# Convolution taps on TensorE from four shifted copies per channel, the output bias on TensorE, dt's weights on four row groups

## The chip, the cores and the metric

The kernel runs on one core of one Trainium2 chip. The metric is the device time of one execution in microseconds; the median of the runs shown is compared. A profile of one execution stands beside the times. Engines are named as in the profile: PE is TensorE's matmul, PEld its weight load, DVE is VectorE, ACT is ScalarE, POOL is GpSimd, and SP is SyncE, which issues nearly all DMAs here, one after the other from one queue.

## The reference

It is one decoder layer in float32 on x of shape (8, 512, 512): a Mamba block, a cross-attention block and a mixture of 32 experts, each followed by an addition and a layer norm. What the change touches is the Mamba block's front and the attention's output:

```python
xz = _layernorm(x) @ in_proj_w                    # 512 -> 2 * 1024
x_main, z = jnp.split(xz, 2, axis=-1)
x_conv = causal_depthwise_conv1d(x_main, conv_w)  # 4 taps per channel, 1024 channels
x_main = silu(x_conv + conv_b)
dt, B, C = jnp.split(x_main @ x_proj_w, [32, 48], axis=-1)
dt = softplus(dt @ dt_proj_w + dt_proj_b)
h_t = exp(A * dt_t) * h_(t-1) + dt_t * B_t * x_t  # 16 states per channel, 512 steps
y = (sum over states of h * C + x_main * D) * silu(z)
out = res_scale * (y @ out_proj_w) + residual
...
attention output: att @ Wo + bo, added to its input
```

The convolution at time t is the sum over k of conv_w[c, k] * x_main[t - 3 + k, c], with zeros before the start of a sequence.

## The kernel before, in words

The program has three parts: `layers` (Mamba, attention, the shared expert and the routing), `experts` and `finish`. `layers` holds a loop over 16 chunks, two of 256 time steps for each of the 8 batches. A chunk has 32 steps (q, g, jj): q counts four groups of 256 channels, g four groups of states, jj two halves. In a step, DVE multiplies dt*x by B (L494), scans along time (L501) and multiplies by C (L510). ACT computes the decays exp(A*dt) for the next step (L480) and copies the state carried in (L488). After the second step of a pair, PE sums the states of both h tiles with four products of 32 columns each into `py` (L521, `fold` is the weight). The h tiles come from a ring of six; a tile is free for its next use when PE has read it.

Everything else is woven into these steps. Chunk i+1's front (its layer norm, transposes, projections, convolution, silu and x_proj) runs at fixed values of k, the step's number in chunk i: norm at 8, transposes at 11, `convolve` at 12, 14, 17 and 20 for q = 0 to 3, silu at 22, x_proj at 23, `prepare` of its first q at 25. The attention and the rest of the previous batch come from a list (`units`), which `work(k)`'s estimates spread over the steps. Each step is cut into thirds. A part may return a rest, which `settle` runs at the next call; `wait` holds it back three thirds. The compiler's scheduler may still reorder instructions on an engine where the data allow it, and the order is fixed when the program is built.

`convolve` projects 256 channels on PE (L343, eight products of 128x256 into PSUM). `first_tap` copies them to the SBUF tile `xp` (L363), which has three columns in front for the previous chunk's tail: POOL clears them (L360) or copies them in (L362), and saves the new tail (L365). ACT then writes the first tap with its bias to `xs` (L369), once for each of two sets of 128 channels. `other_taps` adds three taps to each on DVE (L377, six instructions for a convolution). `xp` is a single tile; `prepare` uses it too, under the name `l`.

`x_proj` (L400) multiplies all channels; `spill` copies the result to `xd` (L406) and sends the B and C rows to DRAM (L408), from where `bcast` spreads them over partitions (L418). `prepare` makes dt: two products of 32 rows (L437), then ACT (L447 to L453) and DVE (L457 to L460). `repeat` spreads dt and dt*x over the partitions by DMA (L428). `pieces` streams the projection weights (L159).

In the attention, `output` multiplies by Wo through `dense` (L750), and `add_up` adds its input (L913) and the bias `bo`, which stands on all partitions (L914). `biases` first folds bv @ Wo into `bo` (L1049).

Of the kernel before, what the change touches and what calls it, by code (L numbers as in the profile page):

```python
# [88 lines left out]
def layers(ctx, tc, a, x1d, filld, based, xbuf):  # L89
# [31 lines left out]
    p2 = ctx.enter_context(tc.tile_pool(name="l_p2", bufs=2))  # L121
    p3 = ctx.enter_context(tc.tile_pool(name="l_p3", bufs=2))
    dp = ctx.enter_context(tc.tile_pool(name="l_dram", bufs=2, space=DRAM))
    psm = ctx.enter_context(tc.tile_pool(name="l_psm", bufs=2, space=PSUM))
    psy = ctx.enter_context(tc.tile_pool(name="l_psy", bufs=1, space=PSUM))
    pss = ctx.enter_context(tc.tile_pool(name="l_pss", bufs=2, space=PSUM))
# [46 lines left out]
    piece = begun(pieces())  # L173
    lnw = const("lnw", [P, DC], a["ln_w"])
    lnb = const("lnb", [P, DC], a["ln_b"])
    cw = const("cw", [P, CC, 4], rows(a["conv_w"]))
    cb = const("cb", [P, CC], a["conv_b"])
    w_x = const("w_x", [P, CC, RANK + 2 * NST], rows(a["x_proj_w"]))
    w_dt = const("w_dt", [RANK, DI], a["dt_proj_w"])
    b_dt = const("b_dt", [P, CC], a["dt_proj_b"])  # L180
    dpar = const("dpar", [P, CC], a["D_param"])
    rs = const("rs", [P, 1], a["res_scale"].partition_broadcast(P))
    bq = cp.tile([P, DC], F32, name="l_bq")
    bk = cp.tile([P, DC], F32, name="l_bk")
    bv = cp.tile([P, DC], F32, name="l_bv")
    bo = cp.tile([P, D], F32, name="l_bo")
    wg = cp.tile([P, DC, E], F32, name="l_wg")

    aneg = cp.tile([P, CC, NQ, NG], F32, name="l_aneg")
# [14 lines left out]
    for at, sign in ((0, 1), (NQ - 1, -1)):  # L204
        nc.gpsimd.affine_select(
            out=fold, in_=fold if at else ones[:, 0:QP], pattern=[[-NQ * sign, QP]], compare_op=ALU.is_ge, fill=0.0,
            base=at, channel_multiplier=sign,
        )
    before = cp.tile([P, P], F32, name="l_before")
    nc.gpsimd.affine_select(  # L210
        out=before, in_=ones, pattern=[[1, P]], compare_op=ALU.is_gt, fill=0.0, base=0, channel_multiplier=-1
# [29 lines left out]
    va = cp.tile([P, SC, NH // 2, 3 * HD], F32, name="l_va")  # L241
    nc.gpsimd.memset(va[:, :, :, HD : 2 * HD], 1.0)

    def big(tag, name):
        return p1.tile([P, SC * (ROW if tag == "s1" else D)], F32, tag=tag, name=name)

    def quad(tag, name):
        return big(tag, name)[:, 0 : DC * S].rearrange("p (c t) -> p c t", c=DC)

# [13 lines left out]
    def later_constants():  # L263

        nc.sync.dma_start(
            aneg.rearrange("p c j g -> p (c j) g"),
            a["A_log"].rearrange("(b c) (s g) -> (c s) b g", c=QP, s=NQ),
        )
        for i in range(NPB):
            for r0 in (HD + 1, 2 * HD + HD + 1):  # L270
                nc.sync.dma_start(
                    kas[i][r0 : r0 + 1, :].rearrange("p (c t) -> p c t", c=DC),
                    ones[0:1, :].unsqueeze(1).to_broadcast([1, DC, P]),
                )
        nc.sync.dma_start(bq, a["bq"])
        nc.sync.dma_start(bk, a["bk"])
        nc.sync.dma_start(bv, a["bv"].rearrange("(c p) -> p c", p=P))
        nc.sync.dma_start(bo, a["bo"].partition_broadcast(P))
        nc.sync.dma_start(wg, rows(a["wg"]))


# [4 lines left out]
    def wait(part):  # L286

        return (clock[0] + 3 if clock else 0), part

    def behind(part):  # L290

# [60 lines left out]
    def convolve(t, q, f):  # L352

        c0 = 2 * q
        ps = project(f, "ps_x")

        def first_tap():
            xp = mp.tile([P, 2, T + 3], F32, tag="xp", name="xp")
            if t == 0:
                nc.gpsimd.memset(xp[:, :, 0:3], 0.0)  # L360
            else:
                nc.gpsimd.tensor_copy(xp[:, :, 0:3], conv_tail[:, c0 : c0 + 2, :])  # L362
            nc.scalar.copy(xp[:, :, 3:], ps)  # L363
            if t < S // T - 1:
                nc.gpsimd.tensor_copy(conv_tail[:, c0 : c0 + 2, :], xp[:, :, T : T + 3])  # L365
            f["xs"][q] = xs = mp.tile([P, 2, T], F32, tag="xs", name="xs", bufs=5)
            for i in range(2):
                c = c0 + i
                nc.scalar.activation(  # L369
                    xs[:, i, :], xp[:, i, 0:T], AF.Identity, bias=cb[:, c : c + 1], scale=cw[:, c, 0:1]  # L370
                )

            def other_taps():
                for i in range(2):
                    acc = xs[:, i, :]
                    for k in range(1, 4):
                        nc.vector.scalar_tensor_tensor(  # L377
                            acc, xp[:, i, k : k + T], cw[:, c0 + i, k : k + 1], acc, ALU.mult, ALU.add
                        )

            return wait(other_taps)

        return first_tap

    def gate_x(q, f):
        if q == 0:
# [10 lines left out]
    def x_proj(f):  # L397
        psd = psm.tile([P, 2, T], F32, tag="mm", name="ps_d")
        for c in range(CC):
            nc.tensor.matmul(  # L400
                psd[0:64, 0, :], w_x[:, c, :], f["xs"][c // 2][:, c % 2, :], start=(c == 0), stop=(c == CC - 1)
            )

        def spill():
            f["xd"] = xd = mp.tile([64, T], F32, tag="xd", name="xd")
            nc.scalar.copy(xd, psd[0:64, 0, :])  # L406
            f["scr"] = scr = dp.tile([2 * NST, T], F32, tag="scr", name="scr")
            nc.sync.dma_start(scr, xd[RANK : RANK + 2 * NST, :])  # L408

        return spill  # L410

# [20 lines left out]
    def prepare(q, f):  # L432

        ps = psm.tile([P, 2, T], F32, tag="mm", name="ps_dt")
        for i in range(2):
            c = 2 * q + i
            nc.tensor.matmul(  # L437
                ps[:, i, :], w_dt[:, c * P : (c + 1) * P], f["xd"][0:RANK, :], start=True, stop=True
            )

        def exponentials():
            u = mp.tile([P, 2, T], F32, tag="u", name="u")
            dt = mp.tile([P, 2, T], F32, tag="dt", name="dt")
# [26 lines left out]

            return wait(both)

        return exponentials
# [10 lines left out]
    def carry(t, q, g, jj):  # L484

        last = state[:, q, g, jj].unsqueeze(2)
        h = mp.tile([P, NB, T + 1], F32, tag="h", name="h", bufs=6)
        nc.scalar.copy(h[:, :, 0:1], last if t else nothing)  # L488
        return h

# [253 lines left out]
            todo.append((3.4, lambda j=j: keys(j), False))  # L744
        return todo

    def dense(lhs, rhs):
        ps = psm.tile([P, S], F32, tag="mm", name="ps_p")
        for dc in range(DC):
            nc.tensor.matmul(ps, lhs(dc), rhs(dc), start=(dc == 0), stop=(dc == DC - 1))  # L750
        return ps

    def units(b):
# [148 lines left out]
        def output(lt):  # L902
# [4 lines left out]
            if lt + 1 < SC:  # L907
                fetch(lt + 1)
            w, attT = loaded["Wo"], st["attT"]
            pp = dense(lambda dc: attT[:, dc, lt * P : (lt + 1) * P], lambda dc: w[:, dc, :])  # L910

            def add_up():
                nc.vector.tensor_tensor(xr, pp, xr, ALU.add)  # L913
                nc.vector.tensor_tensor(st["x2"][lt], xr, bo, ALU.add)  # L914
                if lt == SC - 1:
                    return layernorm(nc, sm, st["x2"], st["x2"], "ln3")

# [113 lines left out]
    def biases():  # L1031
# [12 lines left out]
        for dc in range(DC):  # L1044
# [1 line left out]
            nc.tensor.matmul(  # L1046
                psb, rep[:, dc * P : (dc + 1) * P], loaded["Wo"][:, dc, :], start=(dc == 0), stop=(dc == DC - 1)
            )
        nc.vector.tensor_tensor(bo, bo, psb, ALU.add)  # L1049

    chunks = [(b, t) for b in range(B) for t in range(S // T)]
    steps = [(q, g, jj) for q in range(CC // 2) for g in range(NG) for jj in range(2)]
# [13 lines left out]

    def work(k):

        front = 6.9 if k in (2, 3) else 3.4 if 4 <= k < 8 or k in (12, 14, 17, 20, 23) else 1.0 if k in (11, 25) else 0.0
        return 1.2 + front  # L1070

    f = {"xt": x0}
# [26 lines left out]
    for i, (b, t) in enumerate(chunks):  # L1099
# [7 lines left out]
        for k, (q, g, jj) in enumerate(steps):  # L1107
# [20 lines left out]
            if k == 25 and after:  # L1128
                part(prepare, 0, nf)
            if after:  # L1130
                if k == 8:
                    part(norm_x, nf)
                if k == 11:
                    for j in range(DC // 2):
                        part(flip_x, j, nf)
                if k in (12, 14, 17, 20):
                    part(convolve, after[1], (12, 14, 17, 20).index(k), nf, first=(k == 12))
                if k == 22:
                    parts.append((finish_silu, *nf["xs"].values()))
                if k == 23:  # L1140
                    part(x_proj, nf)
            if side and (k >= 4 or t and k < 2):
# [421 lines left out]
```

## Time and profile before

| what | us |
|---|---|
| median of 3 runs | 5407.47 (5407.45 to 5411.06) |
| the profiled execution's own time | 5406.28 |
| its span from the first to the last instruction | 5404.6 |
| DVE busy in the span | 4235.9 (78%) |
| PE busy in the span | 4672.4 (86%) |
| ACT busy in the span | 2593.6 (48%) |

The mean granted TensorE clock is 0.935. The span falls into the start (to about 57 us), the scan loop (to about 3490), the rest of the last batch (to about 3800), the experts (to about 5340) and the final layer norm. In rows of the groups by line, the numbers after the count are the busy time of the group in us and the mean of one instruction in ns, then the engine's idle time before them and what ended it. In rows of waits they are the total in us, the number of waits and the longest. The busy time of a group counts overlapping instructions once. A float32 product stands as two PE records.

### The profile page before, as it was taken

The numbers are of one execution on the slowest core, as the hardware profiler recorded it, in microseconds if no ns is written. First come the engines' busy times: TensorE is split into PE (matmuls) and PEld (weight loads), VectorE is DVE, ScalarE is ACT, GpSimd is POOL, SyncE is SP. The second block draws the span as 40 slices with busy tenths as digits, with TensorE's granted clock in tenths as the row PEclk, the third lists the DMA queues.
The fourth block names the chain that finished last, engine by engine and source line by source line (L and its number), as shares of the span: only waits on it lengthen the run. The fifth ranks groups of instructions, "written<-read, shape, count | busy, mean of one in ns | idle before, by whom it ended". The sixth has DMA issues, their size and how long they took to land. (4 is left out here: it accounts for less than half of the span.)

```text
span 5404.6 us, 53991 instructions
## 1 busy us (share of the span) xinstructions
PE 4672.4 (86%) x17320; PEld 2476.6 (46%) x17320; DVE 4235.9 (78%) x5369; ACT 2593.6 (48%) x5726; POOL 570.3 (11%) x426
## 2 busy tenths in 40 slices
PE   6768889788888988988888888789999999999994
PEld 3324234234333423433333342333677777777773
DVE  7999899989989989898998998943566555665554
ACT  5566565565656556566565655523222222222223
POOL 1000002002000200200200020011111111111111
PEclk8879989999999999999999999899999999999997
DMA  8875346345444634634544463342344444544544
GB/s 236 266 224 146 87 96 208 81 114 176 114 104 117 197 77 109 189 98 107 174 125 100 117 200 78 91 146 66 103 128 127 123 117 118 127 127 121 129 115 144
DMA packets 486427, 719.03 MB, mean 133 GB/s; under 512 B 117137, under 2 KB 200625, under 8 KB 484096
## 3 DMA queue, kind: packets, MB, share of 16 engines
q1 hardware_dynamic: 450128, 627.16, 41.1%
q0 software_dynamic: 33280, 76.90, 7.5%
q10 hardware_dynamic: 2736, 11.54, 0.5%
q8 instruction: 137, 2.24, 0.2%
q14 instruction: 146, 1.20, 0.1%
HBM read 391.24 MB, written 165.05 MB: 103 GB/s over the span
## 5 line engine op out<-in xcount | busy, mean ns | idle before, releaser
L480 ACT ACTIVATE l_da<-rep,l_aneg 128x256 f32<-128x256 f32 x2048 | 895.0, 501 | 941.8 <-DVE h L501 877.0
L501 DVE TENSOR_TENSOR_SCAN h<-l_da,h 128x1028 f32<-128x1028 f32 x512 | 1166.0, 2292 | 20.3 <-ACT l_da L480 17.7
L494 DVE TENSOR_TENSOR h<-rep,bc 128x1024 f32<-128x1024 f32 x512 | 614.7, 1218 | 103.1 <-PE py L521 84.6
L510 DVE TENSOR_TENSOR h<-h,bc 128x1024 f32<-128x1024 f32 x512 | 619.5, 1217 | 2.1
L521 PE MATMUL py<-h,l_fold 128*32 128x512 f32 x2048 | 368.3, 644 | 113.4 <-DVE h L510 96.5
L813 PE MATMUL ps_s<-l_ka,l_qa 64*128 64x512 f32 x1024 | 325.6, 707 | 137.8 <-DVE mx L815 137.6
L1314 PE MATMUL ps_h<-xT,w 128*128 128x320 f32 x1536 | 435.8, 433 | 0.0
L1394 POOL DMA_INDIRECT based<-y,xe x160 | 255.5, 1597 | 1309.9 <-ACT y L1417 630.0
L1335 DVE TENSOR_TENSOR hT<-ps_h,p 128x320 f32<-128x320 f32 x128 | 62.9, 492 | 378.5 <-PE ps_h L1314 378.5
L815 DVE TENSOR_REDUCE mx<-ps_s 128x2 f32<-128x1024 f32 x256 | 310.2, 1217 | 58.5 <-PE ps_s L813 58.3
L1314 PEld LDWEIGHTS ps_h<-xT,w 128*128 128x128 f32 x1536 | 292.5, 191 | 118.3 <-issue 0.4
L855 PE MATMUL po<-eT,l_va 128*64 128x512 f32 x1024 | 301.5, 670 | 47.6 <-ACT eT L843 43.1
L839 PE MATMUL ps_t<-l_qa,l_ka 64*128 64x512 f32 x1024 | 308.4, 674 | 23.8 <-ACT eT L843 23.1
L843 ACT ACTIVATE eT<-ps_t 128x1024 f32<-128x1024 f32 x256 | 259.0, 1015 | 128.8 <-PE ps_t L839 128.5
L688 POOL DMA_INDIRECT xbuf<-x2t,dest x128 | 217.2, 1697 | 860.4 <-DVE dest L679 760.8
L1314 PE MATMUL ps_h<-t,s 128*128 128x320 f32 x1024 | 286.1, 432 | 0.0
L343 PE MATMUL ps_z<-xnT,wm 128*128 128x256 f32 x1024 | 238.0, 388 | 30.0 <-DVE o L561 24.3
L750 PE MATMUL ps_p<-x2T,wa 128*128 128x512 f32 x512 | 241.5, 626 | 18.1 <-ACT hT L944 10.4
L552 PE MATMUL po<-wm,zs 128*128 128x512 f32 x512 | 244.7, 632 | 13.8 <-DVE z L957 11.9
L343 PE MATMUL ps_x<-xnT,wm 128*128 128x256 f32 x1024 | 246.5, 393 | 4.5 <-ACT xnT L332 2.5
L343 PEld LDWEIGHTS ps_z<-xnT,wm 128*128 128x128 f32 x1024 | 194.6, 193 | 93.0 <-DVE o L561 37.5
L343 PEld LDWEIGHTS ps_x<-xnT,wm 128*128 128x128 f32 x1024 | 196.1, 195 | 80.5 <-issue 43.8
(232 smaller groups left out, 7170.4 us busy)
## 6 DMA issues: line engine op xcount, KB each, us to landing
w<-in_w SPq DMA_DIRECT2D x93, 1024.0 KB
wm<-in_in_proj_w SPq DMA_DIRECT2D x128, 512.0 KB
rep<-dt SPq DMA_DIRECT2D x256, 256.0 KB
rep<-dtx SPq DMA_DIRECT2D x256, 256.0 KB
xbuf<-zero SPq DMA_DIRECT2D x32, 1362.5 KB
xe<-xbuf SPq DMA_DIRECT2D x32, 1362.5 KB
wm<-in_out_proj_w SPq DMA_DIRECT2D x64, 512.0 KB
wa<-in_sw SPq DMA_DIRECT2D x24, 1024.0 KB
```

Source lines behind the costliest of these rows:

```text
L343: nc.tensor.matmul(ps[:, i, :], w[:, dc, i * P : (i + 1) * P], f["xnT"][:, dc, :], start=(dc == 0), stop=(dc == DC - 1),)
L480: nc.scalar.activation(da[:, n, 1:], dt[:, j, i, :], AF.Exp, scale=aneg[:, 2 * q + i, 2 * jj + j, g : g + 1])
L494: nc.vector.tensor_tensor(h[:, :, 1:], dtx.rearrange("p j i t -> p (j i) t"), f["bc", g][0], ALU.mult)
L501: nc.vector.tensor_tensor_scan(flat, da.rearrange("p n t -> p (n t)"), flat, 0.0, ALU.mult, ALU.add)
L510: nc.vector.tensor_tensor(h[:, :, 0:T], h[:, :, 1:], f["bc", g][1], ALU.mult)
L521: nc.tensor.matmul(f["py"][j * QP : (j + 1) * QP, :, :], fold, hs[j // 2][:, 2 * (j % 2) : 2 * (j % 2) + 2, 0:T], start=False, stop=g == N ...
L813: nc.tensor.matmul(ps[:, j, :], qa[r, lt * P : (lt + 1) * P], ka[r, :], start=True, stop=True)
L815: return lambda: nc.vector.tensor_reduce(mx[:, lt, :].unsqueeze(2), ps, AX.X, ALU.max) and None
L839: nc.tensor.matmul(ps[:, j, :], ka[r, kc * P : (kc + 1) * P], qa[r, :], start=True, stop=True)
L843: nc.scalar.activation(eT, ps, AF.Exp)
L855: nc.tensor.matmul(po[j * 2 * HD : (j + 1) * 2 * HD, :], va[:, kc, i, j * HD : (j + 2) * HD], eT[:, j, :], start=(kc == 0), stop=(kc == SC ...
L1314: nc.tensor.matmul(ps, w[:, n, r * P : (r + 1) * P], x[:, n, :], start=not more and n == 0, stop=n == 1, skip_group_check=more,)
```

## The change

The three DVE taps and ACT's first tap of a convolution are replaced. After the copy to `xp`, eight DMAs (`shifted`) make four copies of each channel, shifted by 0 to 3 columns, on four neighbouring partitions: a tile `xk` holds 32 channels times four shifts on its 128 partitions, four times over. Five thirds of a step after that, `summed` multiplies each by a 128x32 matrix that has the four taps of a channel in its column: eight products of 256 columns into PSUM. ACT then adds the bias while it copies the result to `xs`. The matrices are built once at the start: the weights are gathered by partition, multiplied by the 0/1 matrix `fold` and stored in DRAM, and a convolution loads its 128 KB from there.

The output bias becomes a fifth product of `dense`: 32 rows, of which one row of the weight `only` is 1, against rows of `qas[0]`, one of which holds the bias. dt's weights stand on four groups of 32 partitions instead of one, dt's input is copied to all four by three DMAs, and `prepare(q)` uses group q. The ring of h tiles has five tiles instead of six. The front of the next chunk starts a step earlier, and `convolve` runs at 11, 13, 15 and 17.

```diff
-    cw = const("cw", [P, CC, 4], rows(a["conv_w"]))
-    w_dt = const("w_dt", [RANK, DI], a["dt_proj_w"])
+    w_dt = cp.tile([P, 2 * P], F32, name="l_w_dt")
+    for q in range(CC // 2):
+        nc.sync.dma_start(w_dt[q * RANK : (q + 1) * RANK, :], a["dt_proj_w"][:, 2 * q * P : 2 * (q + 1) * P])
...
-    bo = cp.tile([P, D], F32, name="l_bo")
+    bo_row = slice(HD, 2 * HD)
+    only = cp.tile([P, P], F32, name="l_only")
...
+    nc.gpsimd.affine_select(
+        out=only, in_=ones, pattern=[[0, P]], compare_op=ALU.is_ge, fill=0.0, base=1 - 2 * HD, channel_multiplier=1
+    )
+    tapsd = dram1.tile([CC // 2, P, 2 * NQ, QP], F32, name="tapsd")
+    by_tap = big("s1", "by_tap")
+    nc.sync.dma_start(by_tap[:, 0 : DI // QP], a["conv_w"].rearrange("(n c) k -> (c k) n", c=QP))
+    blocks = by_tap[:, D : D + DI].rearrange("p (n m) -> p n m", m=QP)
+    nc.vector.tensor_tensor(
+        blocks,
+        by_tap[:, 0 : DI // QP].unsqueeze(2).to_broadcast(blocks.shape),
+        fold.unsqueeze(1).to_broadcast(blocks.shape),
+        ALU.mult,
+    )
+    nc.sync.dma_start(tapsd.rearrange("q p n m -> p q (n m)"), blocks.rearrange("p (q n) m -> p q (n m)", q=CC // 2))
...
+    def later(part, thirds):
+
+        return (clock[0] + thirds if clock else 0), part
...
         ps = project(f, "ps_x")
-
-        def first_tap():
+        taps = mp.tile([P, 2, NQ, QP], F32, tag="taps", name="taps")
+        nc.sync.dma_start(taps.rearrange("p i j m -> p (i j m)"), tapsd[q].rearrange("p n m -> p (n m)"))
+
+        def shifted():
...
-            f["xs"][q] = xs = mp.tile([P, 2, T], F32, tag="xs", name="xs", bufs=5)
+            xks = []
             for i in range(2):
-                c = c0 + i
-                nc.scalar.activation(
-                    xs[:, i, :], xp[:, i, 0:T], AF.Identity, bias=cb[:, c : c + 1], scale=cw[:, c, 0:1]
-                )
-
-            def other_taps():
-                for i in range(2):
-                    acc = xs[:, i, :]
-                    for k in range(1, 4):
-                        nc.vector.scalar_tensor_tensor(
-                            acc, xp[:, i, k : k + T], cw[:, c0 + i, k : k + 1], acc, ALU.mult, ALU.add
-                        )
-
-            return wait(other_taps)
-
-        return first_tap
+                xk = mp.tile([P, NQ, T], F32, tag="xk", name="xk", bufs=2)
+                for j in range(NQ):
+                    src = xp[j * QP : (j + 1) * QP, i, 0:T]
+                    four = bass.AP(src.tensor, src.offset, [list(src.ap[0]), [1, 4], [1, T]])
+                    nc.sync.dma_start(xk[:, j, :], four)
+                xks.append(xk)
+            return later(lambda: summed(xks), 5)
+
+        def summed(xks):
+            pc = psm.tile([P, 2, T], F32, tag="mm", name="ps_c")
+            for i in range(2):
+                for j in range(NQ):
+                    nc.tensor.matmul(
+                        pc[j * QP : (j + 1) * QP, i, :], taps[:, i, j, :], xks[i][:, j, :], start=True, stop=True
+                    )
+
+            def out():
+                f["xs"][q] = xs = mp.tile([P, 2, T], F32, tag="xs", name="xs", bufs=5)
+                for i in range(2):
+                    nc.scalar.activation(
+                        xs[:, i, :], pc[:, i, :], AF.Identity, bias=cb[:, c0 + i : c0 + i + 1]
+                    )
+
+            return 0, out
+
+        return shifted
...
-            f["xd"] = xd = mp.tile([64, T], F32, tag="xd", name="xd")
-            nc.scalar.copy(xd, psd[0:64, 0, :])
+            f["xd"] = xd = mp.tile([P, T], F32, tag="xd", name="xd")
+            row = p3.tile([P, D], F32, tag="row", name="bcrow")[RANK : RANK + 2 * NST, 0:T]
+            nc.scalar.copy(row, psd[RANK : RANK + 2 * NST, 0, :])
             f["scr"] = scr = dp.tile([2 * NST, T], F32, tag="scr", name="scr")
-            nc.sync.dma_start(scr, xd[RANK : RANK + 2 * NST, :])
+            nc.sync.dma_start(scr, row)
+            nc.scalar.copy(xd[0:RANK, :], psd[0:RANK, 0, :])
+            for r in range(1, CC // 2):
+                nc.sync.dma_start(xd[r * RANK : (r + 1) * RANK, :], xd[0:RANK, :])
...
-            c = 2 * q + i
-            nc.tensor.matmul(
-                ps[:, i, :], w_dt[:, c * P : (c + 1) * P], f["xd"][0:RANK, :], start=True, stop=True
-            )
+            r = slice(q * RANK, (q + 1) * RANK)
+            nc.tensor.matmul(ps[:, i, :], w_dt[r, i * P : (i + 1) * P], f["xd"][r, :], start=True, stop=True)
...
-        h = mp.tile([P, NB, T + 1], F32, tag="h", name="h", bufs=6)
+        h = mp.tile([P, NB, T + 1], F32, tag="h", name="h", bufs=5)
...
-            pp = dense(lambda dc: attT[:, dc, lt * P : (lt + 1) * P], lambda dc: w[:, dc, :])
+            pp = dense(
+                lambda dc: attT[:, dc, lt * P : (lt + 1) * P], lambda dc: w[:, dc, :], (only[bo_row], qas[0][bo_row])
+            )
 
             def add_up():
-                nc.vector.tensor_tensor(xr, pp, xr, ALU.add)
-                nc.vector.tensor_tensor(st["x2"][lt], xr, bo, ALU.add)
+                nc.vector.tensor_tensor(st["x2"][lt], pp, xr, ALU.add)
...
-                if k == 8:
+                if k == 7:
                     part(norm_x, nf)
-                if k == 11:
+                if k == 10:
...
-                if k in (12, 14, 17, 20):
-                    part(convolve, after[1], (12, 14, 17, 20).index(k), nf, first=(k == 12))
+                if k in (11, 13, 15, 17):
+                    part(convolve, after[1], (11, 13, 15, 17).index(k), nf, first=(k == 11))
```

More of the change, by code (lines that the diff above doesn't have):

```diff
@@ L123, in layers @@
     dp = ctx.enter_context(tc.tile_pool(name="l_dram", bufs=2, space=DRAM))
+    dram1 = ctx.enter_context(tc.tile_pool(name="l_dram1", bufs=1, space=DRAM))
     psm = ctx.enter_context(tc.tile_pool(name="l_psm", bufs=2, space=PSUM))
@@ L208, in layers, with big @@
         )
+    nc.gpsimd.affine_select(
+        out=only, in_=ones, pattern=[[0, P]], compare_op=ALU.is_ge, fill=0.0, base=1 - 2 * HD, channel_multiplier=1
+    )
+    def big(tag, name):
+        return p1.tile([P, SC * (ROW if tag == "s1" else D)], F32, tag=tag, name=name)
+    tapsd = dram1.tile([CC // 2, P, 2 * NQ, QP], F32, name="tapsd")
[9 more added lines that the diff above has]
+    nc.sync.dma_start(tapsd.rearrange("q p n m -> p q (n m)"), blocks.rearrange("p (q n) m -> p q (n m)", q=CC // 2))
     before = cp.tile([P, P], F32, name="l_before")
@@ L242, in layers @@
     nc.gpsimd.memset(va[:, :, :, HD : 2 * HD], 1.0)
-    def big(tag, name):
-        return p1.tile([P, SC * (ROW if tag == "s1" else D)], F32, tag=tag, name=name)
     def quad(tag, name):
@@ L277, in later_constants @@
         nc.sync.dma_start(bv, a["bv"].rearrange("(c p) -> p c", p=P))
-        nc.sync.dma_start(bo, a["bo"].partition_broadcast(P))
         nc.sync.dma_start(wg, rows(a["wg"]))
@@ L745, in sources, with dense @@
         return todo
-    def dense(lhs, rhs):
+    def dense(lhs, rhs, more=None):
         ps = psm.tile([P, S], F32, tag="mm", name="ps_p")
         for dc in range(DC):
-            nc.tensor.matmul(ps, lhs(dc), rhs(dc), start=(dc == 0), stop=(dc == DC - 1))
+            nc.tensor.matmul(ps, lhs(dc), rhs(dc), start=(dc == 0), stop=(dc == DC - 1 and not more))
+        if more:
+            nc.tensor.matmul(ps, *more, start=False, stop=True)
         return ps
@@ L1048, in biases @@
             )
-        nc.vector.tensor_tensor(bo, bo, psb, ALU.add)
+        bo = p3.tile([P, D], F32, tag="row", name="bo")[0:1, :]
+        nc.sync.dma_start(bo, a["bo"].unsqueeze(0))
+        nc.vector.tensor_tensor(bo, bo, psb[0:1, :], ALU.add)
+        nc.sync.dma_start(qas[0][2 * HD - 1 : 2 * HD, :], bo)
     chunks = [(b, t) for b in range(B) for t in range(S // T)]
@@ L1067, in work @@
     def work(k):
-        front = 6.9 if k in (2, 3) else 3.4 if 4 <= k < 8 or k in (12, 14, 17, 20, 23) else 1.0 if k in (11, 25) else 0.0
+        front = 6.9 if k in (2, 3) else 3.4 if 4 <= k < 8 or k in (11, 13, 15, 17, 23) else 1.0 if k in (10, 25) else 0.0
         return 1.2 + front
@@ L1130, in layers @@
             if after:
-                if k == 8:
+                if k == 7:
                     part(norm_x, nf)
-                if k == 11:
+                if k == 10:
                     for j in range(DC // 2):
                         part(flip_x, j, nf)
-                if k in (12, 14, 17, 20):
-                    part(convolve, after[1], (12, 14, 17, 20).index(k), nf, first=(k == 12))
+                if k in (11, 13, 15, 17):
+                    part(convolve, after[1], (11, 13, 15, 17).index(k), nf, first=(k == 11))
                 if k == 22:
-                    parts.append((finish_silu, *nf["xs"].values()))
+                    parts.append((lambda f: finish_silu(*f["xs"].values()), nf))
                 if k == 23:
```

## The prediction, made before the changed kernel ran

> **What bounds the kernel now.** I first read the page's two rows of busy tenths, then cut the span into stages with the busy time in stretches.
>
> ```profile
> PE   6768889788888988988888888789999999999994
> DVE  7999899989989989898998998943566555665554
> ...
> 57.00:480.00 423.00, 297.78 (x911) 127.58 (x910) 417.44 (x386) 257.09 (x637) 21.50 (x13) 0.82 0.80 230
> 480.00:3280.00 2800.00, 2370.67 (x8537) 1022.39 (x8535) 2549.49 (x2792) 1652.64 (x3677) 250.43 (x178) 0.93 0.47 129
> 3280.00:3490.00 210.00, 164.78 (x613) 57.85 (x614) 188.69 (x176) 116.89 (x258) 0.00 (x0) 0.90 0.43 103
> 3490.00:3800.00 310.00, 266.38 (x871) 109.02 (x870) 136.20 (x241) 86.13 (x126) 31.90 (x35) 0.91 0.31 104
> 3800.00:5340.00 1540.00, 1533.54 (x6260) 1132.30 (x6260) 895.15 (x1609) 428.53 (x930) 252.37 (x158) 1.00 0.47 116
> ```
>
> The columns of the stretches are: length, busy us of PE, PEld, DVE, ACT and POOL, granted clock, DMA share, GB/s. The change lies in the scan loop (57 to 3490 us) and the start before it; the experts (3800 to 5340) are bound by PE and untouched. In the loop DVE is busy 417.4 + 2549.5 + 188.7 = 3155.6 of 3433 us (92%), PE 2833.2 (83%). To 480 us DVE is all but full; later 8.9% of it is idle. What it idles for is in its waits over the loop:
>
> ```profile
> DVE h L494 <- PE py L521: 84.6, 35, 5.4
> ...
> DVE xs L377 <- ACT xs L369: 27.0, 14, 4.1
> ...
> ACT h L488 <- PE py L521: 106.1, 73, 5.9
> ...
> PE ps_s L813 <- DVE mx L815: 137.1, 94, 4.2
> PE py L521 <- DVE h L510: 95.2, 38, 8.4
> ```
>
> The first row decides what follows. DVE waits for PE's `py` products because a scan's h buffer is free only once PE has read it: six buffers, so DVE runs at most about two pairs of steps ahead of PE. The last two rows show PE waiting for DVE at other places. So the loop is led by DVE, but PE is close behind and the two are tied together. Two stretches of one period of two chunks show how the lead changes: from 1840 to 1960 us DVE is full, from 1960 to 2020 neither engine is:
>
> ```profile
> 1840.00:1960.00 120.00, 99.64 (x366) 40.24 (x366) 116.57 (x109) 74.21 (x167) 6.13 (x4) 0.93 0.42 110
> 1960.00:2020.00 60.00, 50.01 (x177) 16.08 (x174) 46.22 (x39) 27.27 (x57) 0.00 (x0) 0.88 0.31 75
> ```
>
> **The change part by part: what leaves DVE.** From the groups by line:
>
> ```profile
> L377 DVE SCALAR_TENSOR_TENSOR xs<-xp,l_cw,xs 128x256 f32<-128x256 f32 x384 | 164.8, 481 | 42.3 <-ACT xs L369 41.9
> L914 DVE TENSOR_TENSOR x2t<-xr,l_bo 128x512 f32<-128x512 f32 x32 | 21.9, 684 | 0.1
> L521 PE MATMUL py<-h,l_fold 128*32 128x512 f32 x2048 | 368.3, 644 | 113.4 <-DVE h L510 96.5
> ```
>
> Taps: 6 per convolution, 64 convolutions, of which 60 are in the loop: 164.8 x 60/64 = 154.5 us. Their waits in the loop, 27.0 us, go too. Bias additions: 28 of 32 in the loop, 21.9 x 28/32 = 19.2 us; the other 4 are in the tail, where DVE is busy 136 of 310 us, and are worth nothing. Sum: 200.7 us, all on the engine that leads.
>
> **What PE gains.** A convolution now takes eight products, 128 rows deep, 32 columns wide, 256 long. The nearest row is `py`, four products of 32 columns and 512 long (each product is two records); in PE's timeline:
>
> ```profile
> 1791.26 3.60 PE L750 MATMUL ps_p<-wa,cT 128*128 128x512 f32 x8
> 1794.78 1.06 PE L521 MATMUL py<-h,l_fold 128*32 128x512 f32 x8
> 1795.78 3.70 PE L750 MATMUL ps_p<-wa,cT 128*128 128x512 f32 x8
> ```
>
> They take 1.06 us, and over all 256 groups 368.3/256 = 1.44, as some are stretched by a wait between their halves or a slow clock. Eight of 256 stream the same columns: between 1.06 and 1.44, I take 1.2 us, 72 us for 60. The Trainium skill ("TensorEngine Tiling (Array Packing)", Key Properties) speaks against it: a change of tiling mode drains TensorE. Four full-width 128x512 products take 3.6 us, 0.9 each; the group above costs 1.00 us from its start to the next one's, so both its switches together lie inside 1.00 us and need no term of their own. If the four column groups did not run side by side, the eight would cost 8 x 0.45 = 3.6 us (the eight `ps_x` of 256 take 3.62) and 216 us in all; the `py` row speaks against that, so I take 72. Bias: one more 512-long product, 0.9 to 1.0 us, 26 us for 28. `dt` on row groups: same number, same shape; nothing. PE's loop work becomes 2833 + 98 = 2931 us, DVE's 3155.6 - 173.7 = 2982. The engines stand within 2% of each other. A rule that would soften it ("TensorE: Matmul & The Clock Gate", Part 1: idle windows of about 3.4 us halve the clock, busy ones restore it) fits the clocks of the stretches: 0.82 at 70% busy, 0.93 at 85%, 1.00 at 99.6%. At 88% that would return about 0.013 of 2371, 31 us of PE's time. I take none of it, since gaps, not the mean load, decide.
>
> **What is lost by five h buffers and a fuller PE.** No row shows five. Today 35 waits of 84.6 us (2.4 each), all after 480 us; taking away one buffer takes about half a pair of steps (a pair is 13.4 us) from DVE's allowance over PE. Lower bound 0 (the order may put `py` earlier on PE), upper 250 us (each of the 224 pairs after 480 us waiting 1.1 us more). I take that the waits double, +85, as ACT's carry already waits 73 times for the same products, twice as often as DVE.
>
> **DMAs, SP and xp.** Each convolution issues nine transfers of 128 KB (taps, eight shifts), each chunk three more for dt's copies. The `bc` transfers, also 128 KB, cost SP 573 ns each in the median, so 39 x 0.57 = 22 us per chunk; in 2000 to 2210 SP's issues add up to 75 us, so the queue has room. But it is in order: shifts wait for ACT's xp copy and POOL's edge copy (median 1.7 us, up to 4.3), and behind them stand `rep` and the weight pieces. `rep` is already late 33 times for ACT (49.7 us). A `rep` whose issue ended at 1955.99 released ACT at 1959.20, 3.2 us. From xp copy to landing a convolution needs 8 x 0.57 + 3.2 = 8 us or more; five thirds of a step (11 us) are given before PE asks, so PE should mostly not wait. ACT's next write to xp (also `l` of prepare) waits for the shifts to be read. In the first 480 us the DMA engines are 80% busy and get 1.15 MB more per convolution. Bounds 0 and 60; I take +15, near the 16.8 us that DVE waits for `rep` now. ACT has as many convolution operations as before.
>
> **The start.** Before, xp is copied at 17.1 us and the last tap ends at 33.5: 4.1 us per convolution. Now the single xp turns round in 0.6 + 4.6 + 3.2 = 8.4 us, four take 34 and the last product and activation 2 more; the taps must first be gathered in 4-byte pieces, multiplied, stored and loaded, some 5 us. 41 - 16 = +25, bare on the path, as the scans need x_proj's result. Bounds 10 (issues of 0.35 us) and 40.
>
> **The sum.** -200.7 + 85 + 15 + 25 = -76 us. Against the profiled execution (5406.28 us) 5330; the median of the runs is 1.2 us above it, so 5332.
>
> **The rivals.** *PE keeps up.* Products come as early as five buffers ask; only the start and some DMA come back: -201 + 25 + 15 = -161, 5246 us. For it: PE waits for DVE (137.1, 95.2) more than DVE for PE. Against: 2931 beside 2982. Chance 0.22. *The look-ahead becomes the bound: slower.* Every pair of steps needs two h buffers; with five, the second waits for the pair before last, at L494 behind `py`. DVE and PE then take turns, as from 1960 to 2020. With 40 us for start and DMA, the gain is used up when each of 224 pairs waits 161/224 = 0.72 us more; it is 0.38 us now (84.6/224), so a tripling decides. At 1.0 us: +63, 5470 us. For it: balanced loads and a smaller buffer. Against: the first 480 us, which show no such wait. Chance 0.33. *The time freed on DVE turns wholly into waiting*, within 0.2% (11 us, about what a measurement of this kernel can tell from no change): 5407, chance 0.06. The likeliest, 0.39, is 5332, its own range 5290 to 5385.
>
> **How the numbers follow.** Faster is 0.39 + 0.22 = 0.61, same 0.06, slower 0.33. The low end, 5250, keeps nearly all but the best of the first rival; the high end, 5480, takes in the slower case up to 1.05 us per pair.
>
> **What would show it.** Right: no L377, DVE's loop work near 2982 us, the eight products near 1.2 us per convolution, `DVE h <- PE py` near 170 us, the first scan 25 us later, and a loop end earlier by about 75. Wrong: `py` waits of over 250 us, PE waiting for the shifted copies or ACT for xp by more than 50 us in all, eight products taking 3 us, or stretches outside the loop and start that differ.

## The result and the profile after

The changed kernel takes 5587.51 us (median of 4 runs, 5579.95 to 5597.01), the one before 5409.27 beside it: a ratio of 1.033 (95% interval 1.0312 to 1.0349). It is 178 us slower, not 76 faster, and above 5480 us, the upper end of the stated range.

First the page of the changed kernel, its rows of busy tenths:

```profile
PE   6677888888988888888898898889999999999994
DVE  4878888898788888878877888863365655555554
```

Most of DVE's nines of before have become eights. Then the stretches, cut at the first and the last scan (columns as in the prediction), of the kernel before and, below it, of the changed one:

```profile
63.00:3522.10 3459.10, 2859.55 (x10158) 1218.26 (x10156) 3185.39 (x3382) 2043.15 (x4598) 271.93 (x191) 0.92 0.51 138
...
0.00:86.80 86.80, 48.20 (x176) 27.30 (x177) 12.69 (x36) 29.36 (x63) 11.23 (x41) 0.84 0.76 195
86.80:3687.30 3600.50, 3058.75 (x11183) 1271.55 (x11183) 3043.63 (x2989) 2002.61 (x4581) 264.25 (x191) 0.92 0.57 153
```

The start grew by 86.8 - 63.0 = 23.8 us, the loop by 3600.5 - 3459.1 = 141.4, and what follows the last scan by 11.4 (5581.2 - 3687.3 = 1893.9, against 5404.6 - 3522.1 = 1882.5). That is the 176.6 us between the two spans. In the loop DVE's work fell by 142 us, and its idle time rose from 274 to 557. PE's busy time rose by 199 us, and in the end it is the busier engine of the two by a little. The granted clock is 0.92 in both loops, so it is not what makes the difference. Where DVE now waits, in its waits over 57 to 3650 us:

```profile
DVE h L528 <- PE py L555: 147.9, 62, 7.0
DVE mx L851 <- PE ps_s L849: 85.5, 48, 5.3
DVE dtx L491 <- ACT dtx L487: 83.7, 35, 5.1
DVE h L528 <- DMA rep<-dtx: 68.9, 19, 14.4
DVE h L535 <- ACT l_da L514: 30.3, 15, 5.6
```

Before, over the same stretch, the first row had 84.6 us and the last 17.7; the three between:

```profile
DVE mx L815 <- PE ps_s L813: 38.5, 31, 2.8
...
DVE dtx L457 <- ACT dtx L453: 30.2, 23, 3.1
...
DVE h L494 <- DMA rep<-dtx: 16.8, 7, 10.3
```

All have grown: no one wait took the place of the taps. On PE, the groups by line and PE's waits show a new one, and ACT waits for the products in its turn, once for 23.2 us, with all that stands behind them in its order:

```profile
L402 PE MATMUL ps_c<-xk,taps 128*32 128x256 f32 x1024 | 168.3, 420 | 84.6 <-DMA xk<-xp 53.5
...
PE ps_c L402 <- DMA xk<-xp: 50.3, 30, 20.4
...
ACT xs L409 <- PE ps_c L402: 135.5, 36, 23.2
```

168.3/64 = 2.63 us for a convolution's eight products instead of 1.2. In PE's timeline one sees why. In the first row all copies are there (16 records are eight products), in the next two they land while PE works. The last row is one of PE's weight loads in that stretch; each of the eight waits for a copy like this one:

```profile
2184.25 1.07 PE L402 MATMUL ps_c<-xk,taps 128*32 128x256 f32 x16
...
2197.27 2.98 PE L402 MATMUL ps_c<-xk,taps 128*32 128x256 f32 x14 [0.98 <-DMA xk<-xp]
2200.55 0.62 PE L402 MATMUL ps_c<-xk,taps 128*32 128x256 f32 x2 [0.30 <-DMA xk<-xp]
...
2197.54 0.14 PEld L402 LDWEIGHTS ps_c<-xk,taps 128*32 128x32 f32 x2 [0.17 <-DMA xk<-xp]
```

The eight products then take 3.9 us from 2197.27 to 2201.17, each behind its own copy, as SP issues these one after the other (606 ns each in the median), and PE's queue stands meanwhile.

### The profile page after: what moved, and what is told of

Read it like the earlier page. It is cut to its first block, busy times and chain, and to the rows that moved or that the text cites. A ratio compares the mean times of both kernels' runs of the same rounds, so it can differ in the third digit from the quotient of the medians.

```text
span 5581.2 us, 57014 instructions
## 1 busy us (share of the span) xinstructions
PE 4893.0 (88%) x18408; PEld 2531.6 (45%) x18408; DVE 4084.3 (73%) x4954; ACT 2556.0 (46%) x5712; POOL 562.7 (10%) x427
## 5 line engine op out<-in xcount | busy, mean ns | idle before, releaser
L528 DVE TENSOR_TENSOR h<-rep,bc 128x1024 f32<-128x1024 f32 x512 | 612.4, 1215 | 220.9 <-PE py L555 147.9
L849 PE MATMUL ps_s<-l_ka,l_qa 64*128 64x512 f32 x1024 | 346.4, 703 | 95.0 <-DVE mx L851 94.5
L722 POOL DMA_INDIRECT xbuf<-x2t,dest x128 | 197.9, 1546 | 1026.7 <-DVE hT L979 511.9
L363 PE MATMUL ps_x<-xnT,wm 128*128 128x256 f32 x1024 | 258.4, 399 | 7.8 <-DVE k L769 4.1
L402 PE MATMUL ps_c<-xk,taps 128*32 128x256 f32 x1024 | 168.3, 420 | 84.6 <-DMA xk<-xp 53.5
```

The source lines that it names most:

```text
L363: nc.tensor.matmul(ps[:, i, :], w[:, dc, i * P : (i + 1) * P], f["xnT"][:, dc, :], start=(dc == 0), stop=(dc == DC - 1),)
L528: nc.vector.tensor_tensor(h[:, :, 1:], dtx.rearrange("p j i t -> p (j i) t"), f["bc", g][0], ALU.mult)
L849: nc.tensor.matmul(ps[:, j, :], qa[r, lt * P : (lt + 1) * P], ka[r, :], start=True, stop=True)
```

## The experiments

Each ratio is to the kernel before on the same chip. The theories: A, five h tiles shorten DVE's look-ahead (the prediction's slower rival); B, the shifted copies arrive late and hold PE; C, PE's fixed order leads the loop, so DVE's freed time is worth nothing; D, the earlier front crowds full steps.

### The ring of h alone, and the changed kernel without copies

`before_h5`:

```diff
-        h = mp.tile([P, NB, T + 1], F32, tag="h", name="h", bufs=6)
+        h = mp.tile([P, NB, T + 1], F32, tag="h", name="h", bufs=5)
```

> The kernel before with five h tiles instead of six, nothing else. Theory A (the shorter look-ahead is the main cost): DVE's waits for the py products rise from 85 us to well over 150, and the time from 5409 to about 5500 or more. Theory B (the shifted copies arrive late and hold PE in its queue, and the ring of h costs little): within 30 us of 5409.

5416.12 us, ratio 1.0028 (1.0017 to 1.0039). By itself the shorter ring costs 0.3%, as theory B expected, not A. DVE's waits for `py` rise by 37 us, and the time does not follow them:

```profile
DVE h L494 <- PE py L521: 121.2, 60, 5.5
```

`after_nocopy` and `after_nocopy_h6` (the latter with six h tiles); `xk0` is a tile that is filled once at the start:

```diff
-            xks = []
-            for i in range(2):
-                xk = mp.tile([P, NQ, T], F32, tag="xk", name="xk", bufs=2)
...
+            xks = [xk0, xk0]
```

> The changed kernel without the eight shifting DMAs: the products read one tile that is filled once (so the convolution's input is left out), all else as in the changed kernel. Theory B: PE no longer waits for copies, the products take about 1.1 us a convolution instead of 2.6, and the time falls from 5588 to about 5330, what the prediction's sum gives with DMA and start nearly free. Theory A: the five h tiles still bind, and the time stays above 5450.

5512.52 us, 1.0202 (1.0183 to 1.0222).

> The same without the copies, and with six h tiles (the space of one copy tile is free). Theory A: at least 80 us less than the one with five tiles. Theory B: less than 30 us apart; about 5310.

5454.23 us, 1.0095 (1.0078 to 1.0112). Both theories have a part: from 1.033 to 1.0202 the copies account for 1.3% (69 us), from there to 1.0095 the ring of five instead of six for 1.1% (58 us): here it costs several times what it costs in the kernel before. (The loop's granted clock differs too, 0.93 with six tiles and 0.92 with five; how much of the 58 us is the clock's was not separated.) The eight products without copies are as the prediction sized them, 74.8/64 = 1.17 us in the groups by line of `after_nocopy`:

```profile
L398 PE MATMUL ps_c<-l_xk,taps 128*32 128x256 f32 x1024 | 74.8, 408 | 12.6 <-DMA taps<-tapsd 12.5
```

But theory B had expected 5310 to 5330 here, and with six tiles theory A has nothing left to explain. The kernel is still slower than before, with copies and short ring out of the way and the taps gone from DVE. So the gain itself was missing. The loop of `after_nocopy_h6`, and DVE's waits for `py` in it:

```profile
73.00:3548.80 3475.80, 2930.79 (x11157) 1249.78 (x11155) 3038.69 (x2984) 2000.98 (x4578) 242.73 (x191) 0.93 0.52 140
...
DVE h L524 <- PE py L551: 184.6, 70, 10.0
```

DVE works 147 us less than before, and the loop is 17 us longer.

### Copies from ACT's queue, and copies asked for later

```diff
-                    nc.sync.dma_start(xk[:, j, :], four)
+                    nc.scalar.dma_start(xk[:, j, :], four)
```

> The changed kernel with the eight copies issued from ACT's queue instead of SP's. If the copies are late because SP issues them one after the other behind what it waits for (theory B), they start right after ACT's own write of xp, PE's waits for xk fall from 50 us to under 15 and rep is less late; 5480 to 5540, less if ACT's issues cost it little. If the look-ahead is the cost (theory A): within 30 us of 5588.

5806.64 us, 1.0751 (1.0733 to 1.0769): much worse, against both theories. An issue takes ACT as long as SP, in the rows of the tile xk:

```profile
L394 ACTq DMA_DIRECT2D xk<-xp x512: 550/623/2691, 17.9 to 3619.3; - x171
```

512 x 0.623 = 319 us in which ACT can do nothing else, and nearly always the eight of a convolution at a stretch:

```profile
2312.92 6.83 ACTq L394 DMA_DIRECT2D xk<-xp  x8
```

`after_later9`:

```diff
-            return later(lambda: summed(xks), 5)
+            return later(lambda: summed(xks), 9)
```

> The changed kernel with the products nine thirds of a step after the copies are issued instead of five. Theory B for the copies' share (75 us between the changed kernel and the one without copies): the copies are there when PE asks, the products take near 1.1 us a convolution, 40 to 75 us faster than 5588. If their load on SP and the DMA engines is what costs: within 20 us.

5528.0 us, 1.0228 (1.0203 to 1.0253): of the copies' 69 us, 55 come back (1.033 - 1.0228 = 1.0%). The eight products take 102.3/64 = 1.60 us, and ACT's idle time for them falls from 138.9 to 88.2 us in the groups by line. As theory B had it, the copies cost mostly by their lateness, less by their load on SP and the DMA engines.

### What DVE's taps are worth

`before_notaps` drops `other_taps`:

```diff
-            def other_taps():
...
-            return wait(other_taps)
```

> The kernel before without its six DVE taps in each convolution (the convolution keeps its first tap alone), nothing put in their place. Theory C (PE's fixed order leads the loop, and time freed on DVE turns into DVE waiting for PE): within 40 us of the 5405 of before. The prediction's reading (DVE leads, 154.5 us of taps and 27 of waits go): 5220 to 5260.

5444.11 us, 1.0074 (1.0057 to 1.0091): 0.7% slower, with 134 us less of DVE's busy time in the loop. With six h tiles and nothing more on PE, the waits for `py` have doubled:

```profile
61.10:3549.50 3488.40, 2872.21 (x10163) 1213.31 (x10161) 3051.35 (x3022) 2034.38 (x4588) 206.85 (x191) 0.92 0.50 137
...
DVE h L485 <- PE py L512: 173.9, 70, 7.0
```

As the scheduler orders the program anew, `before_tinytaps` keeps every instruction and makes it small:

```diff
-                            acc, xp[:, i, k : k + T], cw[:, c0 + i, k : k + 1], acc, ALU.mult, ALU.add
+                            acc[:, 0:8], xp[:, i, k : k + 8], cw[:, c0 + i, k : k + 1], acc[:, 0:8], ALU.mult, ALU.add
```

> The kernel before with each DVE tap cut from 256 columns to 8 (so most of the convolution is left out): the same instructions with the same dependences, some 100 us less of DVE work, and a build order much nearer to that of before than without the taps. If DVE's freed time is worth something and only the reordering hid it: 40 to 100 us faster than 5404. If DVE's time is slack behind PE (theory C): within 20 us, or slower.

5410.93 us, 1.0011 (0.9998 to 1.0023): no change. In the two traces 88% of DVE's instructions, 84% of ACT's and 96% of PE's stand at the same place in their engine's order. The stretch of its loop, to be held against that of before above:

```profile
60.80:3519.20 3458.40, 2876.52 (x10165) 1225.47 (x10164) 3092.94 (x3382) 2045.55 (x4601) 247.47 (x191) 0.92 0.51 138
```

The loop is 3458.4 us long, as before (3459.1); DVE works 92 us less and waits 92 us more, at the same clock (0.92). Part of these are waits for `py`, which had 84.6 us before:

```profile
DVE h L494 <- PE py L521: 119.2, 46, 5.4
```

`before_taps2` doubles each tap by one that adds zero:

```diff
+                        nc.vector.scalar_tensor_tensor(
+                            acc, xp[:, i, k : k + T], nothing[:, 0, :], acc, ALU.mult, ALU.add
+                        )
```

> The kernel before with every DVE tap followed by a second one of the same size that adds zero: 155 us more of DVE work in the loop. Theory C (PE's order leads from about 480 us on, the taps lie in DVE's slack): up to 80 us slower, of which some 20 in the first two chunks. If DVE leads: 140 us or more.

5508.92 us, 1.0195 (1.0178 to 1.0212). Its loop:

```profile
70.90:3624.70 3553.80, 2911.62 (x10162) 1230.46 (x10160) 3320.69 (x3742) 2027.28 (x4587) 326.43 (x191) 0.91 0.50 134
```

More DVE work does cost: 105 us for the 135 us by which DVE's busy time in the loop grew, more than theory C allowed (80) and less than a leading DVE asked (140). DVE's time is thus no deep slack: the kernel stands near a point from which more work on DVE makes it slower, and less does not make it faster.

### What PE's work is worth

`before_pe` keeps the taps and adds eight products of the change's shape, on constants:

```diff
+            def extra():
+                pc = psm.tile([P, 2, T], F32, tag="mm", name="ps_c")
+                for i in range(2):
+                    for j in range(NQ):
+                        nc.tensor.matmul(
+                            pc[j * QP : (j + 1) * QP, i, :], fold, ones.unsqueeze(1).to_broadcast([P, 2, P]),
+                            start=True, stop=True,
+                        )
```

> The kernel before with its DVE taps, and besides them eight products of 128x32 by 256 columns for each convolution into a PSUM tile of the common ring of two, on constants, read by nobody: PE's share of the change alone, some 70 us of PE. Theory C: the time rises by 50 us or more. If DVE leads: under 20 us.

5467.11 us, 1.0113 (1.0089 to 1.0137): 61 us for 80.9 us of products by the groups by line.

`before_halfz` leaves two of the four products of z's projection out:

```diff
-            for dc in range(DC):
+            n = DC // 2 if name == "ps_z" else DC
+            for dc in range(n):
```

> The kernel before with half the products of the z projection left out (two of four in the sum), so PE has about 110 us less in the loop, spread over four places of each chunk. Theory C: 50 to 100 us faster. If DVE leads: under 25 us faster.

5325.61 us, 0.9856 (0.9839 to 0.9872), 78 us faster, for 100 us of PE's work in the loop:

```profile
60.70:3441.40 3380.70, 2759.53 (x9666) 1123.47 (x9666) 3175.46 (x3382) 2036.86 (x4595) 266.42 (x191) 0.92 0.52 142
```

PE's work is worth some three quarters of its length either way, as theory C has it; on DVE only the way up costs as much. Then both at once, `before_halfz_notaps`:

> Half the z products left out as before, and the six DVE taps too. If the engines lead by turns and PE's share is what hides the taps (theory C): with PE lighter the taps become worth something, 40 us or more below the 5326 of the half alone. If the taps are slack for another reason (the order of the build, latencies): within 20 us of 5326, or above it.

5317.28 us, 0.9842 (0.9819 to 0.9865), and the half alone had 0.9856: the intervals overlap, and the taps, 136 us of DVE's busy time in the loop, are worth 8 us here (29 at the far ends of the two intervals). So theory C's explanation, that PE's load hides the taps, does not hold as it stands: with PE 100 us lighter they are still worth next to nothing. It is not excluded as a part, since with PE at its full load the same deletion cost 0.7%; but there the order of the build differs as well.

`after_halfz`, the same edit in the changed kernel:

> The changed kernel with half the z products left out. Theory C: PE leads the changed kernel more than that before, so at least the 78 us that it gave there: 5588 falls to 5470 to 5510. If the copies or the shorter ring of h lead: less than 50 us.

5525.14 us, 1.0224 (1.0197 to 1.0252), 1.1% or 57 us less than the changed kernel: between what C and the others expected. PE's load is not the whole of what slows it.

### The other parts of the change alone

`before_k` moves the front to the changed kernel's steps:

```diff
-                    part(convolve, after[1], (12, 14, 17, 20).index(k), nf, first=(k == 12))
+                    part(convolve, after[1], (11, 13, 15, 17).index(k), nf, first=(k == 11))
...
```

> The kernel before with the next chunk's front at the steps of the changed kernel (norm at 7, transposes at 10, convolve at 11, 13, 15, 17) and the estimates that go with it, nothing else. Theory D (the earlier, denser front crowds the steps in which PE is full): 30 us or more slower. Otherwise within 15 us.

5430.19 us, 1.0043 (1.0029 to 1.0058), 24 us: between the two marks, so theory D is neither borne out nor refuted.

`before_bias` has the bias as a fifth product, with the change's own lines for it:

```diff
-                nc.vector.tensor_tensor(xr, pp, xr, ALU.add)
-                nc.vector.tensor_tensor(st["x2"][lt], xr, bo, ALU.add)
+                nc.vector.tensor_tensor(st["x2"][lt], pp, xr, ALU.add)
...
```

> The kernel before with the output bias as a fifth product on PE and one DVE addition less for each of the 32 tiles, nothing else. Theory C: no gain, 0 to 30 us slower, for 28 us more of PE. If DVE leads: 10 to 20 us faster.

5437.93 us, 1.0064 (1.0047 to 1.0081). Moving this work to PE loses 32 us, a little more than theory C expected. Between the two profiled spans it is 27 us, and 15 of them lie after the last scan. All kernels with this product, the changed one too, are 11 to 20 us longer there than before, and none of the others by more than 7.

`before_wdt` has dt's weights and its input on four row groups, as in the change:

```diff
+            for r in range(1, CC // 2):
+                nc.sync.dma_start(xd[r * RANK : (r + 1) * RANK, :], xd[0:RANK, :])
...
```

> The kernel before with dt's weights on four row groups and dt's input copied to them (three more DMAs and one more ACT copy a chunk), six h tiles, nothing else: the third part of the change alone, and what the kernel with seven h tiles had besides them. If this part costs by itself, through its DMAs ahead of rep: 20 to 40 us slower than 5405, and the seventh tile is worth nothing either way. If it is free: within 10 us, and the seventh tile cost the 36 us.

5403.07 us, 1.0000 (0.9991 to 1.0010): free.

### A longer ring

With the space that dt's weights leave on four row groups, seven h tiles (`bufs=7`), with whole taps (`before_h7`) and with taps of 8 columns (`before_h7_tiny`):

> The kernel before with seven h tiles instead of six (the space comes from dt's weights on four row groups, with their three more DMAs a chunk). If the ring of h ties DVE to PE: 15 to 60 us faster than 5405, DVE's waits for py under 50 us. If the pace is set elsewhere: within 12 us.

5441.03 us, 1.0064 (1.0047 to 1.0081). The ring tied nothing here: one more tile makes it slower, and as `before_wdt` is free, it is the tile that costs, with the new order that comes with it. The waits for `py` shrink by little. Those for `rep` are longest now, 16.8 us before, in DVE's waits:

```profile
DVE h L498 <- DMA rep<-dtx: 91.4, 33, 4.1
DVE h L498 <- PE py L525: 75.1, 22, 7.0
```

> The same with each DVE tap cut to 8 columns (most of the convolution left out). If the ring of h is what swallows the time that the taps free: 40 us or more below the kernel with seven tiles and whole taps. If hand-offs between the engines in their fixed order do it, whatever the ring's length: within 15 us of it.

5482.46 us, 1.0144 (1.0127 to 1.0161): with the taps small it is slower still, by 41 us, which neither theory expected. That the ring swallows the freed time is refuted for the kernel before. PE is busy 63 us longer in this loop than in that of `before_h7`, with the same products, at a granted clock of 0.91 instead of 0.92; why was not found out.

### The change turned round

If PE's work is what counts, some of it should go to DVE. `before_addD` drops the product by the identity and adds x*D on DVE; for space it takes dt's weights on row groups and gives xs a sixth tile:

```diff
-                nc.tensor.matmul(f["py"], ident, xs, start=True, stop=False)
...
-                    start=False,
+                    start=g == 0,
...
-        f["xs"].pop(q)
+        xs = f["xs"].pop(q)
         pair = f["zs"][:, 2 * q : 2 * q + 2, :]
-        nc.vector.tensor_tensor(pair, pair, f["py"], ALU.mult)
+        nc.vector.tensor_tensor(xs, xs, f["py"], ALU.add)
+        nc.vector.tensor_tensor(pair, pair, xs, ALU.mult)
```

> The change turned round: the kernel before with the product by the identity that adds x*D to py on PE replaced by a DVE addition (64 products of 128x128x512 less, some 68 us of PE; 44 us more of DVE), with dt's weights on four row groups and a sixth xs tile for space. Theory C: faster than before, 5350 to 5390. If DVE leads: 5420 to 5450.

5388.56 us, 0.9967 (0.9955 to 0.9978): 18 us faster than before, just within what theory C expected, and the fastest of the kernels that compute all of the reference. The sixth xs tile was not run alone. Its loop:

```profile
60.40:3505.00 3444.60, 2834.19 (x10043) 1203.96 (x10046) 3222.33 (x3445) 2041.15 (x4610) 258.00 (x191) 0.91 0.51 140
```

DVE works 37 us more, PE 25 less, and the loop is 14.5 us shorter. The product dropped took 78.0 us by the groups by line before, so the rest of PE's work took longer, at a clock of 0.91 instead of 0.92.

## Why the prediction was wrong

**The step that failed: "Sum: 200.7 us, all on the engine that leads".** The taps' and the bias additions' length came out smaller: DVE's busy time in the loop fell by 142 us against 173.7. The instructions overlap their neighbours in the record, and the groups by line count that time twice; over the loop they add up to 199 us more than DVE's busy time before, and to 161 us more after. What the freed time is worth was wrong altogether. Taps of 8 columns gave a ratio of 1.0011, no taps 1.0074, and with half of z left out the taps were worth 8 us: between 92 and 136 us taken from DVE's work brought next to nothing. 92% busy, and full in some stretches, did not mean that less work on DVE shortens the kernel, although more lengthens it. The rows shown beside it pointed that way: 84.6 us of waits for `py`, 106.1 of ACT for the same products, and PE's idle time in its waits for DVE. The prediction named this coupling and then booked the whole of DVE's time as gain, with only a fixed 85 us back.

**"What is lost by five h buffers and a fuller PE", +85.** The row it rests on came out near its figure, `py` waits of 147.9 us where near 170 were expected, but that was luck. The row had 173.9 us in `before_notaps`, with six tiles and no fuller PE, and 184.6 in `after_nocopy_h6`; five tiles alone brought it to 121.2 at 0.3% of the time. So these waits grow mainly as DVE gets less to do, and the freed time spread over the other hand-offs as well: mx, dtx and rep wait too. The prediction's slower rival had the direction, and a tripling of the `py` waits as its condition. It was met neither in that row nor in the time of `before_h5` (1.0028); between the two kernels without copies the shorter ring cost 58 us.

**"What PE gains", 72 us for the products.** Right for the products themselves (1.17 us a convolution against 1.2, with the column groups side by side); wrong in what they are in the kernel, 2.63 us, since PE takes them one by one as the copies land. And their price in time is not nothing: 61 us in `before_pe`. The fuller PE was booked only as part of DVE's waits. The clock returned nothing, as the prediction had assumed: 0.92 in both loops, with PE 83% and then 85% busy.

**"DMAs, SP and xp", +15.** Mis-sized: the copies cost 69 us. The working gave them 8 us of 11, so that "PE should mostly not wait". Four thirds of a step more brought 55 us back, so the margin was too small. In SP's waits, its issues of the copies stand 54.1 us in 39 waits for ACT's copy and once 19.0 us for POOL's, and its other issues come on top.

**"The start", +25: right in size**, 23.8 us by the first scan. Its parts are less sure: in `after_nocopy` the first scan still comes at 74.5 us, 11.5 later than before. In the timeline of the changed kernel's start, ACT's copies to xp stand 10 to 11 us apart, where 8.4 were reckoned and 4 stood before, held by the copies' reads:

```profile
28.02 0.59 ACT L385 COPY xp<-ps_x 128x512 f32<-128x512 f32 x1 [9.05 <-DMA xk<-xp]
...
38.71 0.59 ACT L385 COPY xp<-ps_x 128x512 f32<-128x512 f32 x1 [7.13 <-DMA xk<-xp]
```

**The sum as the runs give it**, in steps of 1%, 54 us: the copies 1.3, the shorter ring in their absence 1.1, and 0.95 for what is left (51 us). By the profiles of before and of `after_nocopy_h6`, 17 us of that lie in the loop, 10 before the first scan and 20 after the last, where `before_bias` lost 15. It holds PE's products (1.1 alone), the bias (0.6), the front's steps (0.4) and some of the start, less whatever the taps gave. Single parts do not add, since each one makes the scheduler order the program anew; no run tells an effect of half a per cent from that of the new order.

**What stays open.** Why DVE's freed time is worth nothing is not settled. Three causes were tested and none is enough: PE's load (with half of z left out the taps are worth 8 us), the length of the ring (seven tiles are slower), and the order of the build as far as `before_tinytaps` keeps it (it still differs in part from before). Nor is it the granted clock, 0.92 in the loops of both. What is left is argued, not shown: steps are chains of hand-offs from PE to DVE to ACT to DVE to PE in a fixed order, and a shorter link in one engine only moves the wait to the next. No run held the order fixed exactly; that wasn't tried.

## What to carry to other kernels

Before work is moved off the busiest engine, make it small in place (here 8 columns of 256) and time that: it gives a first measure of the gain at once (what is left of the instructions and a changed order blur it), and that was zero here at 92% busy. Where two engines wait for each other, a busy share doesn't tell who leads; take a little work from each in turn, and move work towards the one whose relief brings nothing, as `before_addD` did, but little at a time, since more work there can still cost (`before_taps2`). A DMA that feeds an engine with an in-order queue must have landed when the engine comes to it, with all that SP, the copying engine and POOL may be late; pieces that land one by one also take away the side-by-side running of the products that read them.

## What was unexpected of the hardware

Eight 128x32 products of 256 columns ran in 1.07 us when all operands were there, and in 3.9 us when each waited for its own copy. A DMA issue of 128 KB took ACT's queue 623 ns in the median, no less than SP's 606, and eight of them for each convolution cost the kernel 4% more (1.0751 against 1.033).
